# One SBUF tile shared from layer 0 to the tokens, whitening's sums taken in layer 0's last batch, 28 output stores, and keys written in order

## The chip, the cores and the metric

The kernel runs on one core of a Trainium2 chip. A core has TensorE (PE), VectorE (DVE), ScalarE (ACT), GpSimd (POOL) and SyncE (SP), each with its own instruction stream, and 16 DMA engines that the streams feed through queues; nearly all transfers here are issued by SP. The metric is the time of one execution on the device in microseconds. The kernel before takes 7492.99 us, the median of 3 runs between 7485.9 and 7499.06 us.

## The reference, cut to what matters

The input is 8 images of 56x56 pixels with 128 channels, all float32, and four layers follow one another:

```python
# layer 0: deformable convolution and an MLP, both with residuals
xp = x @ w_in + b_in
h = gelu(batch_norm(depthwise3x3(x)))
offset = h @ w_off + b_off ; mask = softmax(h @ w_msk + b_msk)
x = x + gamma1 * layer_norm(dcn(xp, offset, mask) @ w_out + b_out)
x = x + gamma2 * layer_norm(gelu(x @ w_fc1) @ w_fc2)
# layer 1: whitening. The flat activations become 64 rows; every 9th column is a sample
x1 = transpose(x).reshape(64, -1) ; x1_s = x1[:, ::9]
cov = x1_s @ x1_s.T / n_cols + 0.01 * eye(64)
y = isqrt_newton_schulz(cov, 5) @ (x1 - mean(x1_s))
# layer 2: attention (8 heads of 16, keys = queries = values) and 64 experts
t = t + attn(layer_norm(t)) ; t = t + experts(layer_norm(t))
# layer 3: linear attention and 64 experts
```

In layer 1 the reference names the array's axes N, C, H, W although they hold 8, 56, 56 and 128. So "rows of a block" are image rows: the 64 rows of `x1` gather image rows of all eight images, and nothing of the covariance is known before all of layer 0 has its result.

## The kernel before, in words

**Layer 0, first stage** (`conv_layer`, L127). Its instructions stand in the order they are written in (`manual_schedule`). For each image it loads the pixels (`xs`), transposes them, projects them (`pj`), filters them, and stores the projected strips to DRAM; one image later it computes the offsets and masks `om` from `hT` and stores them (L337); one image after that `ranged` (L341) runs ReLU over the offsets twice, once for each sign, into the scratch tile `over`, and gathers whether any offset is beyond 1 (`far`). After eight images one flag `near` is read, and an `If` takes the sampler for near offsets.

**Layer 0, second stage** (`sample_near`, L413). The loop over `g` has `LEN = PH + 5 = 12` ticks for each image. The MLP of the current image goes through a pipeline of six steps, one strip row `r` (of seven) a tick: `project` in tick r, ..., `combine` in tick r + 5. Beside it the next image's samples are made. In the last batch there is no next image. After the last strip of an image `by_patch(..., store=True)` writes the image to `z` in DRAM in 8 stores (L757). `z` is kept as [row, image, column, channel]. The big buffers of this stage (`wide`, `wT`, `hat`, `even`, `smp`) are tiles of their own.

**Layer 1** (`whiten_layer`, L1019). 14 loads bring all of `z` into `x` [128, 25088]: partition p < 64 holds the first half of row p of `x1`, partition 64 + p the second half. PE transposes samples (`p_smp`, L1063), DVE copies them, PE multiplies them into `cov` (L1073), and DVE sums the samples for the mean (`tot`, L1051). Then come `a` (L1094), its norm, five Newton-Schulz steps of 64x64 matmuls with copies on DVE (L1119 to L1129), and the subtraction of the mean from `x` in seven pieces of 3584 columns (L1140). For each piece PE multiplies by `both`, a block diagonal of two copies of the result (L1146), DVE and ACT copy the products to `o`, and 16 stores write it to `y` (L1157), each with 8 partitions that lie 8 apart, because neighbouring rows of a block go to different images.

**Token constants** (`token_layers`, L2663): weights are loaded and transposed, and `key_bound` (L2616) bounds the scores of layer 3.

**Keys** (`attention_keys`, L1191). The order here is the scheduler's. Zeros are written to the two DRAM arrays `sel_d` in 8 stores on ACT's queue (L1205). For each image the tokens `t` are loaded (L1166), normalised (`bn_stats` L1223, `rsqrt`, `normalize` L111), transposed to `xT` (L120), multiplied into the keys `kT` (two stores, L1250) and the values `va` (two stores, L1266); GpSimd squares the values, and DVE finds the largest norm, `tops`. From this `low` and the flag `small` follow, and the attention (`attend`, L1424) starts after the flag is read by all engines.

The change replaces these lines in the stage order:

```python
        # whiten_layer, before
        for c in range(0, WHALF, WC):
            for h in range(2):
                nc.sync.dma_start(
                    x[h * WB : (h + 1) * WB, c : c + WC],
                    zf[:, h * WHALF + c : h * WHALF + c + WC],
                )
        # attention_keys, before
        for sel in sels:
            rows = sel.rearrange("(r s) o -> r (s o)", s=S)
            for a in range(0, n_b * E, 128):
                nc.scalar.dma_start(rows[a : a + 128], zero)
```

Of the kernel before, what the change touches and what calls it, by code (L numbers as in the profile page):

```python
# [126 lines left out]
def conv_layer(tc, k, x, w, z):  # L127
# [3 lines left out]
    with ExitStack() as ctx:  # L131
# [7 lines left out]
        q.om = dp.tile([n_batch, T, NT, 3 * GP], F32, name="om_d")  # L139

# [36 lines left out]
        far = cp.tile([T, 2 * n_batch], F32, name="far")  # L177
        near = cp.tile([1, 1], I32, name="near")
        with ExitStack() as pre:
# [57 lines left out]
            xss, accs = {}, {}  # L237

            def load(n):
                xss[n] = hp.tile([T, NT, C], F32, name="xs")  # L240
                nc.sync.dma_start(
                    xss[n],
                    x[n].rearrange("h w c -> (h w) c").rearrange("(t p) c -> p t c", p=T),
                )
# [65 lines left out]
            def activated(n):  # L310
                hT = hp.tile([C, PH, PX, T // NX, NX], F32, name="hT")
                a4 = accs.pop(n).rearrange("p (a r) (b s) -> p r a b s", r=PH, s=PX)
                for r in range(PH):
                    nc.scalar.activation(
                        hT[:, r].rearrange("p s a b -> p a b s"),
                        a4[:, r],
                        AF.Gelu,
                        bias=bn_t,
                        scale=bn_s,
                    )  # L320
                return hT
# [18 lines left out]
            def ranged(n, om):  # L340
                for i, sign in enumerate((1.0, -1.0)):  # L341
                    over = ip.tile([T, NT, 2 * GP], F32, name="over")
                    nc.scalar.activation(
                        over,
                        om[:, :, : 2 * GP],
                        AF.Relu,
                        bias=minus1,
                        scale=sign,
                        accum_out=far[:, 2 * n + i : 2 * n + i + 1],
                    )  # L350

            with tc.manual_schedule(engines=None):
                load(0)
                oms = {}
                for n in range(n_batch + 2):
                    if n + 1 < n_batch:
                        load(n + 1)
                    if n < n_batch:
                        pj = hp.tile([IH, IW, C], F32, name="pj")
# [8 lines left out]
                    if n > 1:  # L368
                        ranged(n - 2, oms.pop(n - 2))
                    if 0 < n <= n_batch:  # L370
# [13 lines left out]
        with both.Else():  # L384
            with tc.For_i(0, n_batch) as n:
                sample_any(tc, k, q, x, n)

# [25 lines left out]
def sample_near(tc, k, q, n_batch):  # L413
# [4 lines left out]
    with ExitStack() as ctx:  # L418
# [11 lines left out]
        wide = bp.tile([T, NT * WS], F32, name="wide")  # L430
# [4 lines left out]
        wT = bp.tile([KP, T, GRP, NT], F32, name="wT")  # L435
# [11 lines left out]
        even = wp.tile([C, C], F32, name="even")  # L447
# [11 lines left out]
        def weights(n):  # L459
# [6 lines left out]
            for r0 in range(0, PH, 2):  # L466
# [4 lines left out]
                hat = rp.tile([T, 2, NP, 2 * PX, 3, GRP], F32, name="hat")  # L471
                hat = hat[:, :, :, :n_t]
# [203 lines left out]
        blocks = (1, 1, 1, 2, 2)  # L676
        for g in range(LEN * n_batch):
            n, tick = divmod(g, LEN)
            more = n + 1 < n_batch
            if more and tick == 2:  # L680
# [19 lines left out]
            if five:  # L700
                fn, r = five
                combine(xts[fn][:, r], p5, rs5, xts[fn][:, r])
                if r == PH - 1:
# [26 lines left out]
            if left > 1:  # L730
                sample(n + 1, m + 16)

# [76 lines left out]
def sample_any(tc, k, q, x, n):  # L809

    nc = tc.nc
    with ExitStack() as ctx:
# [12 lines left out]
        xt = bp.tile([T, PH, GT, C], F32, name="xt")  # L825
        by_patch(nc, q.x[n], xt)
        zt = bp.tile([T, PH, GT, C], F32, name="zt")
# [191 lines left out]
def whiten_layer(tc, k, z, y):  # L1019

    nc = tc.nc
    n_half = -(-WCOLS // WSTEP) // 2
    first = (0, -WHALF % WSTEP)
    n_tr = -(-n_half // 128)
    WC = 7 * 512
    zf = z.rearrange("h n w c -> (h n w c)").rearrange("(r s) -> r s", r=WB)
    with ExitStack() as ctx:
# [4 lines left out]
        ps1 = ctx.enter_context(tc.tile_pool(name="l1p1", bufs=1, space=PSUM))  # L1032
        ps2 = ctx.enter_context(tc.tile_pool(name="l1p2", bufs=2, space=PSUM))


        x = bp.tile([2 * WB, WHALF], F32, name="x")
        for c in range(0, WHALF, WC):
            for h in range(2):
                nc.sync.dma_start(
                    x[h * WB : (h + 1) * WB, c : c + WC],  # L1040
                    zf[:, h * WHALF + c : h * WHALF + c + WC],
                )


        smp = bp.tile([128, 2 * n_tr * WB], F32, name="smp")
        cov = ps1.tile([WB, WB], F32, name="cov")
        tot = bp.tile([2 * WB, 1], F32, name="tot")
        n_mm = 0
        for h in range(2):
            rows = slice(h * WB, (h + 1) * WB)  # L1050
            nc.vector.tensor_reduce(  # L1051
                tot[rows],
                x[rows, first[h] : first[h] + WSTEP * (n_half - 1) + 1 : WSTEP],
                AX.X,
                ALU.add,
            )
            for i0 in range(0, n_tr, 8):
                p = ps.tile([128, 8, WB], F32, tag="m", name="p_smp")
                m = min(8, n_tr - i0)
                for i in range(i0, i0 + m):  # L1060
                    n = min(128, n_half - i * 128)
                    a = first[h] + i * 128 * WSTEP
                    nc.tensor.transpose(  # L1063
                        p[:n, i - i0, :],
                        x[rows, a : a + WSTEP * (n - 1) + 1 : WSTEP],
                        k.ident[rows, rows],
                    )
                for i in range(i0, i0 + m):
                    n = min(128, n_half - i * 128)
                    at = (h * n_tr + i) * WB  # L1070
                    s = smp[:n, at : at + WB]
                    nc.vector.tensor_copy(s, p[:n, i - i0, :])
                    nc.tensor.matmul(  # L1073
                        cov, s, s, start=(n_mm == 0), stop=(n_mm == 2 * n_tr - 1)
                    )
                    n_mm += 1

        n_smp = float(2 * n_half)
        fold = bp.tile([2 * WB, 2, WB], F32, name="fold")
        for h in range(2):  # L1080
            nc.vector.tensor_tensor(
                fold[:, h], k.ident[:, :WB], k.ident[:, WB:], ALU.add
            )
        p = ps.tile([2 * WB, 1], F32, tag="m", name="p_mean")
        nc.tensor.matmul(
            p, fold.rearrange("p a b -> p (a b)"), tot, start=True, stop=True
        )
        mean = bp.tile([2 * WB, 1], F32, name="mean")
        nc.vector.tensor_scalar(mean, p, 1.0 / n_smp, None, ALU.mult)

        a = bp.tile([WB, WB], F32, name="a")
        ieps = bp.tile([WB, WB], F32, name="ieps")
        nc.vector.tensor_scalar(ieps, k.ident[:WB, :WB], WEPS, None, ALU.mult)
        nc.vector.scalar_tensor_tensor(a, cov, 1.0 / n_smp, ieps, ALU.mult, ALU.add)  # L1094


# [4 lines left out]
        ones = bp.tile([WB, WB], F32, name="ones")  # L1101
        nc.vector.memset(ones, 1.0)
        p = ps.tile([WB, 1], F32, tag="m", name="p_norm")
        nc.tensor.matmul(p, ones, ssum, start=True, stop=True)
        norm = bp.tile([WB, 1], F32, name="norm")
        nc.scalar.activation(norm, p, AF.Sqrt)
        inv = bp.tile([WB, 1], F32, name="inv")
        nc.vector.reciprocal(inv, norm)
        rinv = bp.tile([WB, 1], F32, name="rinv")
        nc.scalar.activation(rinv, norm, AF.Sqrt)  # L1110
        nc.vector.reciprocal(rinv, rinv)
        i15 = bp.tile([WB, WB], F32, name="i15")
        nc.vector.tensor_scalar(i15, k.ident[:WB, :WB], 1.5, None, ALU.mult)
        ym = sp.tile([WB, WB], F32, tag="ym", name="ym")
        nc.vector.tensor_scalar(ym, a, inv, None, ALU.mult)
        zm = k.ident[:WB, :WB]
        for _ in range(WITER):
# [4 lines left out]
            p = ps2.tile([WB, WB], F32, tag="ns", name="p_y")  # L1122
            nc.tensor.matmul(p, ym, tm, start=True, stop=True)
            ym = sp.tile([WB, WB], F32, tag="ym", name="ym")
            nc.vector.tensor_copy(ym, p)
# [4 lines left out]
        dm = bp.tile([WB, WB], F32, name="dm")  # L1130
        nc.vector.tensor_scalar(dm, zm, rinv, None, ALU.mult)
        both = bp.tile([2 * WB, 2 * WB], F32, name="both")
        nc.vector.memset(both, 0.0)
        nc.vector.tensor_copy(both[:WB, :WB], dm)
        p = ps2.tile([2 * WB, WB], F32, tag="ns", name="p_low")
        nc.tensor.matmul(p[WB:], k.ident[:WB, :WB], dm, start=True, stop=True)
        nc.vector.tensor_copy(both[WB:, WB:], p[WB:])

        for c in range(0, WHALF, WC):
# [13 lines left out]
            for h in range(2):  # L1153
                k_, off = divmod(h * WHALF + c, IW * C)
                for b in range(NB):
                    row, n = divmod(7 * b + k_, NB)
                    nc.sync.dma_start(  # L1157
                        y[n]
                        .rearrange("(a r) w c -> r a (w c)", r=7)[row][:, off : off + WC],
                        o[h * WB + b : (h + 1) * WB : NB],  # L1160
                    )
# [29 lines left out]
def attention_keys(tc, k, w, yv, kT_out, va_out, low, bias, small, sels):  # L1191


# [3 lines left out]
    n_b = yv.shape[0]  # L1197
    with ExitStack() as ctx:
        cp = ctx.enter_context(tc.tile_pool(name="akc", bufs=1))
        zero = cp.tile([128, S], F32, name="edge")  # L1200
        nc.gpsimd.memset(zero, 0.0)
        for sel in sels:
            rows = sel.rearrange("(r s) o -> r (s o)", s=S)
            for a in range(0, n_b * E, 128):
# [1678 lines left out]
```

## Time and profile before

| What | us | Where it is read |
|---|---|---|
| median of 3 runs (lowest, highest) | 7492.99 (7485.9, 7499.06) | times |
| the profiled execution: its own time, its span | 7509.97, 7508.2 | times, page |
| layer 0, first stage | 0 to 395 | timeline |
| flag, weights and `om` of image 0 | 395 to 460 | timeline |
| layer 0, second stage | 460 to 1460 | timeline |
| last image to `z`, `z` to `x`, covariance | 1460 to 1545 | timeline |
| Newton-Schulz and subtraction | 1545 to 1567 | timeline |
| products and 112 stores | 1567 to 1684 | timeline |
| constants, first tokens, statistics | 1684 to 1740 | timeline |
| keys and values of 8 images | 1740 to 2052 | timeline |
| attention and all that follows | 2052 to 7508 | timeline |

The chain of work that ended last runs mostly through the attention: 54% of the span is PE, and the three costliest lines of the chain (L1527, L1587, L1603) are the attention's. The stages that the change touches lie before 2052 us, and each ends before the next begins: the covariance needs the last image, the stores need the matrix, the tokens need the last store, and the attention needs the flag from the last keys. In the views below "start, us" is the begin and length of an instruction or a group of equal ones; "x112" counts them; SPq and ACTq are the instructions with which SP and ACT issue transfers, so their time is the time of issuing, which is long when the queue is full.

### The profile page before, as it was taken

The page shows a single profiled execution, that of the slowest core. Times are in us where ns is not written, and L with a number is a line of the kernel's source. Part 1 is how long each engine was busy: PE and PEld are TensorE (multiplying, and loading weights), DVE is VectorE, ACT ScalarE, POOL GpSimd, SP SyncE. Part 2 cuts the span into 40 slices and gives each one's busy share as a digit, 9 for nine tenths or more (in the row PEclk, how much of TensorE's full clock was granted, in tenths as well). Part 3 has the DMA queues.
Part 4 walks back from the last instruction along what each step waited for, and adds up shares of the span by engine and source line. Part 5 has one row for each costly group of instructions (what it writes and reads, how often), then busy time and mean ns, then how long its engine had stood idle before and what let it go on. Part 6 is the DMA issues. An engine that isn't in the chain of part 4 may idle for free.

```text
span 7508.2 us, 162711 instructions
## 1 busy us (share of the span) xinstructions
PE 6513.2 (87%) x63686; PEld 3041.6 (41%) x63686; DVE 4668.4 (62%) x8268; ACT 4337.6 (58%) x5268; POOL 3898.1 (52%) x3925
## 2 busy tenths in 40 slices
PE   7938888745699999998999998999998999689668
PEld 5626556423433333332333333333333333267326
DVE  5757775126756677676777676776675777446542
ACT  4525455302277777776777776777776776424320
POOL 0003233202267677667666767767766767335650
PEclk8858888866799999999999999999998999789775
DMA  5533435346467677766777766767765767752227
GB/s 134 140 68 72 87 73 95 65 107 233 189 158 187 164 164 190 168 165 153 175 165 177 178 162 142 191 160 177 179 162 135 190 161 181 206 175 89 78 87 223
DMA packets 721075, 1126.49 MB, mean 150 GB/s; under 512 B 106225, under 2 KB 472514, under 8 KB 711362
## 3 DMA queue, kind: packets, MB, share of 16 engines
q1 hardware_dynamic: 676946, 1073.74, 58.5%
q10 hardware_dynamic: 39248, 37.88, 1.5%
q8 instruction: 513, 8.40, 0.5%
q0 software_dynamic: 4096, 4.24, 0.2%
q14 instruction: 272, 2.23, 0.1%
HBM read 292.59 MB, written 193.65 MB: 65 GB/s over the span
## 4 chain that ended last, share of the span: by engine, by line
PE 54%; POOL 7%; DMA 4%; DVE 3%; issue 2%; SPq 1%; ACT 1%; ACTq 0%; POOLq 0%; DVEq 0%
PE p_s L1527 20%; PE av L1587 15%; PE p_t L1603 11%; POOL t_all L1578 3%; POOL t_all L1573 2%; PE p_s L2340 1%; DVE t_all L1562 1%; DMA room<-in_L_ffn_weight_dram 1%; PE p_qk L2409 1%; PE p_o L1665 1%; DMA sel_d<-vals,row 1%; SPq L1575 1%; PE p_g L1714 1%; DMA t_all<-t_all 1%; POOL xn L2545 1%
## 5 line engine op out<-in xcount | busy, mean ns | idle before, releaser
L1538 ACT ACTIVATE room<-p_s,bias 128x1024 f32<-128x1024 f32 (+2 forms) x3008 | 3142.1, 1102 | 1153.3 <-PE p_s L1527 1149.7
L1562 DVE STREAM_TRANSPOSE t_all<-room 128x1024 f32<-128x1024 f32 x1920 | 2246.7, 1217 | 751.1 <-ACT room L1538 293.1
L1578 POOL COPY t_all<-t_all 32x1024 f32<-32x1024 f32 x1920 | 1988.7, 1036 | 104.1
L1527 PE MATMUL p_s<-t_all 32*128 32x512 f32 x10752 | 1647.6, 642 | 14.6 <-DMA t_all<-kT_d 13.7
L1573 POOL COPY t_all<-t_all 32x1024 f32<-32x1024 f32 x960 | 995.7, 1037 | 1142.0 <-DVE t_all L1562 857.4
L1527 PEld LDWEIGHTS p_s<-t_all 32*128 32x128 f32 x10752 | 502.5, 183 | 1147.3 <-issue 512.4
L1587 PE MATMUL av<-room,vas 128*32 128x512 f32 (+1 forms) x7616 | 820.0, 518 | 5.1 <-issue 3.3
L1587 PE MATMUL av<-room 128*32 128x512 f32 (+1 forms) x6208 | 663.1, 516 | 1.9 <-issue 1.2
L1603 PE MATMUL p_t<-t_all,vas 128*32 128x256 f32 x8064 | 546.8, 389 | 47.4 <-POOL t_all L1578 45.1
L1603 PE MATMUL p_t<-t_all,room 128*32 128x256 f32 x7296 | 492.3, 387 | 39.4 <-POOL t_all L1578 29.7
L1603 PEld LDWEIGHTS p_t<-t_all,vas 128*32 128x32 f32 x8064 | 215.0, 110 | 503.9 <-issue 249.4
L1603 PEld LDWEIGHTS p_t<-t_all,room 128*32 128x32 f32 x7296 | 194.3, 109 | 455.3 <-issue 235.8
L1587 PEld LDWEIGHTS av<-room,vas 128*32 128x32 f32 x7616 | 204.6, 111 | 216.2 <-issue 112.6
L512 PE MATMUL p_w<-ident,wide 112*88 112x112 f32 x896 | 152.3, 316 | 132.4 <-DVE wide L502 84.3
L581 POOL TENSOR_TENSOR rsy<-rsy,mhalf 112x4 f32<-112x4 f32 x56 | 58.0, 1035 | 386.2 <-DVE rsy L580 386.2
L1587 PEld LDWEIGHTS av<-room 128*32 128x32 f32 x6208 | 160.0, 110 | 187.1 <-issue 105.4
L1622 DVE TENSOR_TENSOR acc<-acc,p_t 128x256 f32<-128x256 f32 x320 | 132.4, 414 | 134.0 <-PE p_t L1603 131.7
L431 POOL MEMSET wide<- 112x10416 f32 x1 | 8.8, 8777 | 394.4 <-DMA om_d<-om 394.4
L512 PEld LDWEIGHTS p_w<-ident,wide 112*88 112x88 f32 x896 | 124.8, 172 | 201.5 <-issue 131.5
L618 PE MATMUL p_f<-x1T,w 128*128 128x448 f32 x448 | 189.2, 565 | 16.9 <-ACT sqm L565 13.7
L514 ACT COPY wT<-p_w 88x448 f32<-88x448 f32 x152 | 137.2, 924 | 114.1 <-PE p_w L512 114.1
L306 DVE SCALAR_TENSOR_TENSOR acc<-xp,dw,acc 128x3136 f32<-128x3136 f32 x56 | 195.2, 3485 | 2.0
(369 smaller groups left out, 8585.2 us busy)
## 6 DMA issues: line engine op xcount, KB each, us to landing
t_all<-t_all SPq DMA_DIRECT2D x4800, 128.0 KB
px<-strips SPq DMA_DIRECT2D x64, 616.0 KB
room<-in_L_ffn_weight_dram SPq DMA_DIRECT2D x30, 1024.0 KB
room<-in_L_ffn_weight_dram SPq DMA_DIRECT2D x120, 256.0 KB
va_d<-va SPq DMA_DIRECT2D x16, 1600.0 KB
kT_d<-kT SPq DMA_DIRECT2D x16, 1568.0 KB
t_all<-kT_d SPq DMA_DIRECT2D x96, 256.0 KB
vas<-va_d SPq DMA_DIRECT2D x52, 256.0 KB
```

The lines of the kernel that those rows point to most:

```text
L306: nc.vector.scalar_tensor_tensor(acc, view(j), dw[:, j : j + 1], acc, ALU.mult, ALU.add)
L512: nc.tensor.transpose(p[:, g], around[:, :, g], k.ident[:T, :T])
L514: copy(wT[:, :, :, t].rearrange("k a g -> k g a"), p)
L618: nc.tensor.matmul(p, q.w1[:, f * 128 : (f + 1) * 128], x1T, start=True, stop=True)
L1527: nc.tensor.matmul(ss[j // 2][:m, j % 2, u * width : (u + 1) * width], key_tile(b.n, b.g, t, j), q[32 * j : 32 * j + 32], start=True, stop ...
L1538: nc.scalar.activation(e[:m, :, cols], s[:m, :, cols], AF.Exp, bias=bias[:m])
L1562: nc.vector.transpose(x[:, :, a, 2 * h : 2 * h + 2].rearrange("p q h b f -> p (h b) q f"), e.rearrange("p h (b q f) -> p (h b) q f", b=4, ...
L1573: nc.gpsimd.tensor_copy(dst, src)
L1578: nc.gpsimd.tensor_copy(into[r, u], x[r, u])
L1587: nc.tensor.matmul(av[32 * j : 32 * j + 32, :width], value_tile(b.n, b.g, t, j), es[j // 2][:m, j % 2, u * width : (u + 1) * width], start ...
L1603: nc.tensor.matmul(p[32 * j : 32 * j + 32, : QB // 2], value_tile(b.n, b.g, 4 * b.j + c, j), yt[:, :, :, j, c].rearrange("p q a f -> p a q ...
L1622: nc.vector.tensor_tensor(to, to, p, ALU.add)
```

## The change: what it does

- One tile `arena` [128, 25088] lives from layer 0 to the end. It holds `pj`, `xs` and one `hT` in the first stage, `wide`, `wT`, `hat` and `even` in the second, whitening's `x`, the buffers of keys and values, and then the tokens `t_all`. `ranged` works in place on the offsets: Abs, then ReLU with the bias of -1.
- The zeros for `sel_d` are written in the first stage, one store with each of the images 1 to 8, on SP's queue, from a tile of 448 columns read seven times.
- A class `WhitenSums` replaces the first half of whitening. In ticks 0 to 3 of the last batch SP issues the loads of images 0 to 6 from `z` into `arena` (56 loads of 8 rows, of 28672 or 14336 bytes a row). Image 7 is not stored; `take` moves its strip rows from `xt` to `arena` from SBUF to SBUF after each `combine` (8 transfers, 16 for r = 3). In ticks 6 to 11 `more` transposes the samples of one column group at the start of the tick and multiplies those of the group before into `cov`, which has a 65th column of ones so that it holds the sums too. The last group and the copy to `sums` follow the loop.
- `whiten_layer` is called after the token constants. It subtracts the mean as before, drops the last `p_y`, copies `ym` on ACT, and permutes the output rows with `order`, so that one store covers m images: 28 stores, four for each piece, of 8m neighbouring partitions to (m, 8) places in DRAM, m between 1 and 7.
- `attention_keys` stands in written order. The statistics of image n + 1 are taken among the groups of image n, the normalisation is split between DVE and ACT, four `kT` buffers take turns, the values are made in groups of four tiles with the squares on ACT, and the tokens of image n + 2 are loaded at the end of image n, after its two key stores.

```diff
 def ranged(n, om):
-    for i, sign in enumerate((1.0, -1.0)):
-        over = ip.tile([T, NT, 2 * GP], F32, name="over")
-        nc.scalar.activation(
-            over,
-            om[:, :, : 2 * GP],
-            AF.Relu,
-            bias=minus1,
-            scale=sign,
-            accum_out=far[:, 2 * n + i : 2 * n + i + 1],
-        )
+    part = om[:, :, : 2 * GP]
+    nc.scalar.activation(part, part, AF.Abs)
+    nc.scalar.activation(
+        part, part, AF.Relu, bias=minus1, accum_out=far[:, n : n + 1]
+    )
...
                     if n > 1:
                         ranged(n - 2, oms.pop(n - 2))
+                    if 0 < n and edges:
+                        rows = edges.pop().rearrange("r (a b) -> r a b", b=QC)
+                        nc.sync.dma_start(
+                            rows, empty.unsqueeze(1).to_broadcast([128, S // QC, QC])
+                        )
...
+        sums = WhitenSums(tc, k, q)
         for g in range(LEN * n_batch):
             n, tick = divmod(g, LEN)
             more = n + 1 < n_batch
+            if not more:
+                for i in range(2 * tick, min(2 * tick + 2, n_batch - 1)):
+                    sums.fetch(i)
+                if tick == 5:
+                    sums.begin(pst, "t", xp, "px")
+                if tick > 5:
+                    sums.more(ps, "m", tick - 6)
...
-                if r == PH - 1:
+                if fn == n_batch - 1:
+                    sums.take(fn, r, xts[fn][:, r])
+                elif r == PH - 1:
                     by_patch(nc, q.z[fn], xts.pop(fn), store=True)
...
+        sums.more(ps, "m", PH - 1)
+        sums.end()
+class WhitenSums:
+    def place(self, r, n):
+        return r + (r + n) // PH, (r + n) % PH
+    def fetch(self, n):
+        for r in range(PH):
+            for rows, at, a, m in self.parts(n, r):
+                self.nc.sync.dma_start(
+                    self.x[rows, at : at + m], self.q.zr[r, n][:, a : a + m]
+                )
...
+    def more(self, ps, tag, col):
+        for group in self.pieces((col + 1) * IW * C):
+            p = ps.tile([128, 7, WB], F32, tag=tag, name="p_smp")
+            for i, (h, a, last, n) in enumerate(group):
+                rows = slice(h * WB, (h + 1) * WB)
+                nc.tensor.transpose(
+                    p[:n, i], self.x[rows, a:last:WSTEP], self.k.ident[rows, rows]
+                )
+            nc.vector.tensor_copy(s[:n, :m, :WB], p[:n, :m])
+            self.add()
+            self.waiting.append((s, group))
...
 # whiten_layer
             for h in range(2):
-                k_, off = divmod(h * WHALF + c, IW * C)
-                for b in range(NB):
-                    row, n = divmod(7 * b + k_, NB)
-                    nc.sync.dma_start(
-                        y[n]
-                        .rearrange("(a r) w c -> r a (w c)", r=7)[row][:, off : off + WC],
-                        o[h * WB + b : (h + 1) * WB : NB],
-                    )
+                col, off = divmod(h * WHALF + c, IW * C)
+                cut = h * WB + 8 * (7 - col)
+                for lo, hi, n, at, j in (
+                    (cut, (h + 1) * WB, 0, col, 0),
+                    (h * WB, cut, col + 1, 55 * (col + 1) + col + 2, 5),
+                ):
+                    m = (hi - lo) // 8
+                    if m:
+                        dst = yu[at : at + 55 * m].rearrange("(n j) e -> n j e", j=55)
+                        nc.sync.dma_start(
+                            dst[:, j : j + 50 : 7, off : off + WC], o[lo:hi]
+                        )
...
 # attention_keys, under manual_schedule
+        load(0)
+        load(1)
+        for g in range(NG):
+            sums(0, g)
+        roots(0)
+        xn = norm(0, 0)
+        for n in range(n_b):
+            for g in range(NG):
+                turn(xn, xT, g)
+                if g:
+                    keys(n, xT, g - 1)
+                if g + 1 < NG:
+                    xn = norm(n, g + 1)
+                sums(n + 1, g)
+                if g > 1:
+                    values(n, xT, 4 * (g - 2), square)
+            roots(n + 1)
+            keys(n, xT, NG - 1)
+            values(n, xT, 4 * (NG - 2), square)
+            if n + 1 < n_b:
+                xn = norm(n + 1, 0)
+            values(n, xT, 4 * (NG - 1), square)
+            load(n + 2)
+            for g in range(2):
+                nc.sync.dma_start(va_out[n, g], vas[n % 2][:, g].rearrange("p t j d -> p (t j d)"))
```

## The prediction

> **What bounds the kernel now.** I read four views. The page first: its chain of waits and costliest groups belong to the attention (L1527, L1587), whose instructions the change leaves as they are. From the first read of `small` on, all five engines have the same sequence in both programs, so what is won or lost falls before 2052 us and stays. Then the timeline of the same 2052 us, for the anchors; then the windows, for what each stage is full of; then the groups of single lines. Timeline (start, length, instruction):
>
> ```profile
> 394.82 0.34 SPq L337 DMA_DIRECT2D om_d<-om  x1
> 1371.21 97.77 SPq L757 DMA_DIRECT2D z<-xt  x13
> 1472.51 29.26 SPq L1039 DMA_DIRECT2D x<-z  x14
> 1576.33 104.44 SPq L1157 DMA_DIRECT2D y<-o  x112
> 1688.76 7.58 SPq L1166 DMA_DIRECT2D t<-y  x2
> ```
>
> Each of these releases the next stage. The windows (length, busy time of PE, PEld, DVE, ACT, POOL with counts, clock, DMA share, GB/s):
>
> ```profile
> 1424.00:1460.00 36.00, 32.10 (x147) 19.68 (x145) 8.53 (x34) 16.74 (x29) 10.98 (x10) 0.99 0.01 2
> 1460.00:1536.00 76.00, 10.72 (x72) 8.62 (x72) 9.84 (x39) 0.00 (x0) 0.00 (x0) 0.50 0.91 191
> 1567.00:1685.00 118.00, 53.56 (x100) 22.12 (x100) 15.17 (x26) 15.99 (x28) 0.00 (x0) 0.73 0.45 112
> 1685.00:1740.00 55.00, 3.65 (x10) 1.63 (x10) 17.73 (x127) 0.00 (x0) 19.51 (x9) 0.50 0.84 296
> 1800.00:2045.00 245.00, 171.22 (x703) 114.85 (x701) 189.66 (x602) 69.40 (x166) 61.61 (x12) 0.78 0.56 207
> ```
>
> The reader is to see four things. The last MLP ticks are PE's (32 of 36 us) while DMA is idle. Bringing `z` to `x` is DMA's (0.91). The stage of the 112 stores is limited by transfers of 112 GB/s, although the engines' share is only 0.45. In the keys DVE is the fullest (190 of 245 us).
>
> **The change part by part.** Anchors are of the profiled execution (its own time 7509.97 us; span 7508.2). It lies 17 us above the median of the runs; I add the sum to that median.
>
> *First stage.* The eight zero stores have 0.3 to 1 us of issue each on SP and 1.6 MB; in the page's first two slices DMA is half idle (5 and 5 tenths), a load is issued one image ahead of use, and on ACT's queue each took 4.97 us. Cost 0; without that cover 8 x 5 = 40 us. `ranged` for image 7 used to run beside the store of `om`, which lands at 401.3. In place it must wait for it: 401.3 + Abs 1.97 + ReLU 1.97 + 0.2 + 1.0 for the flag = 406.5, against 400.0, with the `If` released at 401.3 before: **+5 to +6.5 us**, I take 6.5.
>
> *Fetch.* SP issues it after image 6's last store (1378.5 + 6.5 = 1385). It is 11.24 MB, 8 partitions a transfer, 8 apart. The nearest row is `y<-o`: same partitions, same row length, 12.8 MB in 107 us (1576 to 1684) = 121 GB/s at 8 packets in flight. So 93 us, to 1478. Bounds: 213 GB/s, as `x<-z` with 64 partitions, gives 53 us; 107 GB/s gives 105. Queued behind it on SP is `take` of strip 0, 2 us, and its landing. PE meets `more(0)` at the head of tick 6, 1417.2 + 6.5 = 1424; its transposes wait for that landing, and behind them on PE stand all matmuls of ticks 6 to 11, and ACT, DVE and POOL behind those. PE goes on at about 1484 (bounds 1444, 1496): 60 us of wait in a stage where it was busy.
>
> *Rest of the batch.* From tick 6 to the last `combine` is 42.2 us in the trace (1417.2 to 1459.5). I add 3 for the clock, which rows after a pause show at 0.50 for 4 to 10 us; 9 for 44 transposes (0.17 to 0.25 each) and their passes (0.11 to 0.31 each) now on PE's path; 7.5 for waits on `take` (about 2 us landing at some of the six ticks, twice at the 16 transfers of r = 3); 12.5 for the last `take`, `more` and the copy. Sums ready at 1484 + 42 + 3 + 9 + 7.5 + 12.5, rounded 1560. Before, `cov` was ready at 1543.8. The removed 8 stores (9.5 us), 14 loads (59 us) and `tot` (two of 5.1 us) are thus more than eaten up by the wait: **+16**.
>
> *Constants.* They ran in the shadow of the last stores and of the tokens' loads (1680.9 to 1693.8); now, on DVE, `kb_top` and `bound` stand ahead of `a` in the queue, and the loads only start after the `If`. Same chain: 12.9 us, plus 15 small DVE copies of 0.15 to 0.2 = 16. `a` at 1577 (before 1545.5). Newton and the seven subtractions (2.07 us each, now interleaved alike) 22 us; last `p_y` gone, 1 us: first product at 1599, first store at 1608 (before 1576.3): **+32 in all so far**.
>
> *Stores.* The same 12.85 MB in 896 rows of 14336 B. No row shows a transfer to (m, 8) places. Lower bound: 16 packets in flight at the 420 GB/s of `kT` would be 31 us, then PE's 47 us for 49 products (53.6 busy) decides. Nearest row: `y<-o` itself, 107. Upper: packets in flight followed the outer count in every row that I can see (8 for `y<-o`, 14 for `z<-xt`, 16 for 64 partitions). The outer count here is m, from 1 to 7, so if it holds a store keeps m streams of 8 rows: 24 stores x 8 + 4 x 1 = 196 rows one after another on the first stream, at 535 ns (fastest packet) 105 us, at 914 (mean) 179. I take 125: fewer streams meet than in `y<-o`, so packets run at some 640 ns, nearer the fast end. Landed at 1608 + 125 + 2 = 1735, before 1684.
>
> The Trainium skill ("DMA: Bandwidth & Descriptors", section "Why a DMA increments its semaphore by 16 and not by 1") says that a queue spreads a transfer over the largest k up to 16 that divides the slowest non-1 dimension of both sides, on the lowest-numbered engines. The trace's 8, 14 and 16 agree. By it the first engine would carry 196 rows and the stage takes 105 us or more; the row of `y<-o` alone would give 107, and thus some 18 us less in the total than my sum.
>
> *First tokens.* Before: 1684 to 1740 for constants, two loads and edges that shared the queue (`sel_d` 33 us, the first statistics at 1707, the first transpose at 1740.2). Now only the load (8.5), 28 x 0.26 = 7.3 of statistics, 5.3 for the root on POOL, 0.7: first transpose at 1735 + 22 = 1757, before 1740.2. So 34 of the lost us come back here: **+17**.
>
> *Keys.* Before 311 us from the first transpose to `low`, 38 an image. New, image by image: from the last key (E) the two key stores take 7.8 us on the DMA engines, the tokens of image n + 2 lie behind them (7.2 + 2), so they land at E + 17. DVE runs in order: it has some 7 us of work, then meets their `bn_stats`, and `norm` and the keys of the next group stand behind those. Then six groups at 3.2 us (DVE: 4 x 0.26, 2 x 0.31, 0.68, half a copy and the gaps), then `ms` waits 6.3 us for the root on POOL (4.80) with the last key copy behind it: 17 + 19 + 6.3 = 43 an image (bounds 39 and 47). The first image needs no late load, 27.5; the last 34.5. 27.5 + 6 x 43 = 286, + 34.5 = 320, against 311: **+9**. What is saved, GpSimd's squares and seven small value copies, lies beside DVE and is worth nothing while this wait stands; without it an image takes 32 us.
>
> Sum: 6.5 + 9.5 (sums at 1560) + 16 (constants) + 18 (stores) + 1 (landing) - 34 + 9 = +26; 7493 + 27 = **7520 us**.
>
> **Rivals.** *A, the stores run wide.* All 16 streams, PE decides: 47 instead of 125, -78: 7442. For it: 8m neighbouring partitions, as the loads with 64 have 16 in flight. Against: the destination's outer count. *B, the load is not late, on the other side.* The mechanism is only the keys' DVE wait: it goes if the tokens land by E + 7, that is if the loads of 7.2 us overlap the key stores rather than follow; 32 an image, -66: 7454. It decides alone once an image is under 39 us (-24 or more). For it: the DMA share in the keys is 0.56, and two images are held. Against: one queue, where the trace's `t<-y` issued after stores took them in order. *C, fetch at the rate of `x<-z`:* -40, 7480. *D, packets meet:* 179 for the stores, or 47 an image: +54 or +24, 7545 to 7574. *E, nothing gained or lost:* stores as before (107) and an image at 42: -24, 7496, within what a measurement can tell.
>
> **How the numbers follow.** Forecast as summed (7508 to 7550): 0.43. A 0.12, B 0.14, C 0.08, D 0.15, E 0.08. A measurement of this kernel can tell some 0.2%, 15 us, from no change (the runs before spread by 13). Faster: A, B and half of C, 0.30. Same: E, and the other half of C, 0.12. Slower: 0.58. Range: A's 7442 and two small gains together at the low end, D at the high: 7430 to 7590; the likeliest case's own is 7505 to 7560.
>
> **What would show it.** In the profile after: a PE gap of about 60 us at the head of tick 6, with the transposes of `p_smp` behind a DMA (right), or none over 20 (C); `a` some 30 us later; 28 stores over 105 to 160 us with few packets in flight, or under 60 (A); DVE waiting for `t<-y` some 10 us in each image, with images 43 us apart, or 32 (B). I would be wrong most easily in the stores' rate and in the keys, where two waits in order on DVE are worked out and not seen.

## The result, and the profile after

The changed kernel takes 7540.41 us (median of 5 runs, 7533.65 to 7554.67) against 7496.19 for the kernel before in 5 runs (7485.9 to 7503.89): slower by 44 us, a ratio of 1.0063 with a 95% interval from 1.0048 to 1.0077. The forecast was 7520, 24 above that median. The profiled execution has a span of 7537.9 us.

The timeline of SP, whose transfers release the stages (start, length, instruction):

```profile
380.83 0.34 SPq L360 DMA_DIRECT2D om_d<-om  x1
393.03 3.39 SPq L911 DMA_DIRECT2D xt<-in_x_dram  x8
1369.99 82.71 SPq L808 DMA_DIRECT2D arena<-z  x54
1453.35 106.21 SPq L817 DMA_DIRECT2D arena<-xt  x64
1612.01 93.33 SPq L1276 DMA_DIRECT2D y<-o  x28
1731.95 4.37 SPq L1283 DMA_DIRECT2D t<-y  x2
```

The reader is to see that SP issues the loads of images 0 to 6 until 1452.7 and only then the 64 strip transfers of image 7 (`arena<-xt`, until 1559.6), where PE was to finish layer 0 beside them. The strips fill 106 us although one takes 0.70 to 0.89 us to issue: between the rows SP waits for the next `combine`. The timeline of PE shows at each column group what the head of the tick waited for (in brackets: idle before, and what ended it):

```profile
1466.67 0.92 PE L870 MATMUL p_smp<-ident,arena 64*128 64x64 f32 x6 [57.94 <-DMA arena<-xt]
1480.96 0.87 PE L870 MATMUL p_smp<-ident,arena 64*128 64x64 f32 x6 [0.60 <-DMA arena<-xt]
1495.01 0.92 PE L870 MATMUL p_smp<-ident,arena 64*128 64x64 f32 x6 [3.39 <-DMA arena<-xt]
1514.52 0.57 PE L870 MATMUL p_smp<-ident,arena 64*128 64x64 f32 x3 [5.84 <-DMA arena<-xt]
1531.70 0.92 PE L870 MATMUL p_smp<-ident,arena 64*128 64x64 f32 x6 [2.56 <-DMA arena<-xt]
1546.49 0.92 PE L870 MATMUL p_smp<-ident,arena 64*128 64x64 f32 x6 [6.12 <-DMA arena<-xt]
1561.99 0.92 PE L870 MATMUL p_smp<-ident,arena 64*128 64x64 f32 x6 [10.55 <-DMA arena<-xt]
```

One wait of 57.9 us, and then one in every tick, because the strip that the tick needs was made by the tick before. SP's timeline between 1486 and 1494 us shows what that takes for one strip:

```profile
1486.14 6.50 SPq L817 DMA_DIRECT2D arena<-xt  x8
```

The eight transfers are issued from 1486.1 to 1492.6, and PE goes on at 1495.0, 8.9 us after the first; for the 16 transfers of r = 3 it is 12.9 us (1501.6 to 1514.5). The windows (columns as before: length, busy time of PE, PEld, DVE, ACT, POOL, clock, DMA share, GB/s) show both, then the stores and the keys:

```profile
1412.00:1467.00 55.00, 0.33 (x3) 0.36 (x4) 0.00 (x0) 0.00 (x0) 0.00 (x0) 0.50 0.43 109
1467.00:1566.00 99.00, 69.94 (x313) 47.85 (x312) 14.82 (x50) 18.30 (x31) 13.14 (x12) 0.71 0.06 15
1612.00:1732.00 120.00, 44.14 (x83) 18.19 (x81) 12.45 (x18) 13.66 (x24) 11.76 (x6) 0.69 0.29 107
1790.00:2055.00 265.00, 152.32 (x632) 93.69 (x632) 145.97 (x507) 107.62 (x226) 28.77 (x6) 0.77 0.52 183
```

In the first row PE, DVE, ACT and POOL stand still. In the second PE's clock is 0.71, where the same ticks before had 0.99. The stores move 107 GB/s, with less DMA share than before. In the keys DVE is no longer full (146 of 265 us, before 190 of 245), and yet the stage takes longer. The view of waits between 1780 and 2090 us (waiter, what it waited for, total us, times, longest) says why:

```profile
DVE st L1351 <- DMA t<-y: 64.6, 6, 10.9
DVE ms L1360 <- POOL rs L1472: 34.9, 7, 5.0
```

By anchors, forecast against measured, in us:

| Step | forecast | profile after |
|---|---|---|
| first transposes of layer 0, against 37.39 before | no change | 29.16 |
| last `om` store to weights of the second stage (before 6.65) | 13.2 | 12.2 |
| PE's wait at tick 6 | 60 | 57.9 |
| from its end to the sums | 74 | 99.6 |
| sums to `a` | 16 | 14.3 |
| `a` to the first store | 31 | 31.4 |
| first store to the tokens' load | 127 | 119.9 |
| from there to the first transpose of the keys | 22 | 25.8 |
| first transpose to `low` and `small` (before 311.6) | 320 | 333.6 |

`small` is set at 2091.3, before at 2051.8: 39.5 later. Counted from the last `om` store (380.83, before 394.82) it is 53.5 later. The rest, the same instructions, took 9.8 less in this execution. Such differences are scatter: in profiles of kernels with an equal first stage the last `om` store is issued between 380.3 and 400.6. So steps are compared here by the distance of two anchors, and kernels by the ratios of their runs.

### The profile page after: what moved, and what is told of

Same layout as the page of the kernel before. It is cut to its first block, busy times and chain, and to the rows that moved or that the text cites. A ratio compares the mean times of both kernels' runs of the same rounds, so it can differ in the third digit from the quotient of the medians.

```text
span 7537.9 us, 162656 instructions
## 1 busy us (share of the span) xinstructions
PE 6507.4 (86%) x63686; PEld 3026.0 (40%) x63686; DVE 4601.4 (61%) x8052; ACT 4396.2 (58%) x5368; POOL 3863.1 (51%) x3918
## 5 line engine op out<-in xcount | busy, mean ns | idle before, releaser
L1739 DVE STREAM_TRANSPOSE arena<-room 128x1024 f32<-128x1024 f32 x1920 | 2246.7, 1217 | 744.0 <-ACT room L1715 351.5
L1755 POOL COPY arena<-arena 32x1024 f32<-32x1024 f32 x1920 | 1993.7, 1038 | 104.3
L1704 PE MATMUL p_s<-arena 32*128 32x512 f32 x10752 | 1649.8, 643 | 17.1 <-DMA room<-va_d 16.2
L1750 POOL COPY arena<-arena 32x1024 f32<-32x1024 f32 x960 | 997.8, 1039 | 1126.8 <-DVE arena L1739 869.0
L1704 PEld LDWEIGHTS p_s<-arena 32*128 32x128 f32 x10752 | 502.9, 184 | 1152.6 <-issue 520.0
L1780 PE MATMUL p_t<-arena,vas 128*32 128x256 f32 x8064 | 546.9, 389 | 44.6 <-POOL arena L1755 41.3
L1780 PE MATMUL p_t<-arena,room 128*32 128x256 f32 x7296 | 492.7, 387 | 37.6 <-POOL arena L1755 23.6
L1780 PEld LDWEIGHTS p_t<-arena,vas 128*32 128x32 f32 x8064 | 215.0, 109 | 500.5 <-issue 247.0
L1780 PEld LDWEIGHTS p_t<-arena,room 128*32 128x32 f32 x7296 | 194.6, 109 | 456.2 <-issue 243.7
L552 PE MATMUL p_w<-ident,arena 112*88 112x112 f32 x896 | 151.6, 315 | 132.9 <-DVE arena L542 81.5
L554 ACT COPY arena<-p_w 88x448 f32<-88x448 f32 x152 | 137.1, 923 | 111.2 <-PE p_w L552 111.2
## 6 DMA issues: line engine op xcount, KB each, us to landing
arena<-arena SPq DMA_DIRECT2D x4800, 128.0 KB
```

The lines of the kernel that those rows point to most:

```text
L552: nc.tensor.transpose(p[:, g], around[:, :, g], k.ident[:T, :T])
L554: copy(wT[:, :, :, t].rearrange("k a g -> k g a"), p)
L1704: nc.tensor.matmul(ss[j // 2][:m, j % 2, u * width : (u + 1) * width], key_tile(b.n, b.g, t, j), q[32 * j : 32 * j + 32], start=True, stop ...
L1739: nc.vector.transpose(x[:, :, a, 2 * h : 2 * h + 2].rearrange("p q h b f -> p (h b) q f"), e.rearrange("p h (b q f) -> p (h b) q f", b=4, ...
L1750: nc.gpsimd.tensor_copy(dst, src)
L1755: nc.gpsimd.tensor_copy(into[r, u], x[r, u])
```

## The experiments

The theory is the forecast's own: PE's wait for the loads, strips that land too late, DVE's wait for late tokens and the constants on the path cost more than the change saves, and the stores gain nothing. The rivals are that transfers set the end wherever PE's instructions stand, that behind each wait another stands, and that the stores' shape is at fault. All ratios are to the kernel before on the same chip; the changed kernel's is 1.0063. A gain over the changed kernel, given in us, is the difference of two such ratios, and with their intervals it is sure to some 16 us either way.

### All transposes behind the loop

```diff
-                if tick > 5:
-                    sums.more(ps, "m", tick - 6)
...
-        sums.more(ps, "m", PH - 1)
+        for i in range(PH):
+            sums.more(ps, "m", i)
```

> The transposes and covariance passes of all seven column groups stand behind the loop instead of at the head of ticks 6 to 11. If PE's wait for the loads (57.9 us at tick 6) and the seven waits for strips that come only after the tick before (some 33 us of the 99.6 from there to the sums) are the cost, the MLP ends near 1451 as before, the 64 strip transfers follow the loads on SP at 0.77 us each, 1453 to 1502, and the sums are ready near 1512 instead of 1566: 50 us faster than the changed kernel, 7490. Rival: the transfers set the end whatever PE does; then the sums stay within 10 us of 1566 and the time at 7535.

Ratio 0.9995 (0.9979 to 1.001), 51 us below the changed kernel, and the sums at 1521.9. SP's timeline:

```profile
1371.15 84.55 SPq L807 DMA_DIRECT2D arena<-z  x56
1456.82 58.22 SPq L816 DMA_DIRECT2D arena<-xt  x64
```

The loads take as long as before. The strips now go out back to back, 58 us instead of 106, since their contents are ready. The order of PE's queue was worth 51 us. The sums were expected at 1512: the strips took 58 us where 49 were put. SP's 64 strips now stand last before the sums, which the run with image 7 by way of DRAM puts to the test.

### One tick later

```diff
-                if tick > 5:
-                    sums.more(ps, "m", tick - 6)
+                if tick > 6:
+                    sums.more(ps, "m", tick - 7)
...
-        sums.more(ps, "m", PH - 1)
+        for i in range(PH - 2, PH):
+            sums.more(ps, "m", i)
```

> The transposes of column group c stand at the head of tick c + 7 instead of c + 6, the last two groups behind the loop; the transfers are as in the changed kernel. This tells the one long wait (57.9 us) from the seven landings. PE still meets the loads, one tick on, and waits some 48 us there, but each strip then has a whole tick to land. If the landings that come right after the tick's own combine are the larger part, the sums are ready near 1525, as in the run with all groups behind the loop (1521.9), ratio 1.000. Rival: the long wait is what is lost, and hardly less of it here; then the sums stay near 1555, ratio 1.005.

Ratio 1.0011 (0.9997 to 1.0025): 39 of the 51 us come back although the long wait stays. PE's timeline:

```profile
1473.85 0.92 PE L871 MATMUL p_smp<-ident,arena 64*128 64x64 f32 x6 [52.80 <-DMA arena<-xt]
1486.21 0.90 PE L871 MATMUL p_smp<-ident,arena 64*128 64x64 f32 x6
1495.64 0.90 PE L871 MATMUL p_smp<-ident,arena 64*128 64x64 f32 x6
1512.78 0.87 PE L871 MATMUL p_smp<-ident,arena 64*128 64x64 f32 x6 [0.80 <-DMA arena<-xt]
1520.02 0.92 PE L871 MATMUL p_smp<-ident,arena 64*128 64x64 f32 x6 [4.51 <-DMA arena<-xt]
1526.66 0.92 PE L871 MATMUL p_smp<-ident,arena 64*128 64x64 f32 x6 [4.23 <-DMA arena<-xt]
```

52.8 us of waiting still stand at the head, but the next ticks have no wait before them; two waits of 4.5 and 4.2 us are left, ahead of the last two groups. From the end of the long wait to the sums it is 57 us (1473.9 to 1531.1) instead of 99.6, and the clock over it is 0.83 instead of 0.71. So the strips' issue and landing within a tick are the larger part of what could be had by moving `more` alone; the long wait's time is mostly not to be had that way, because without it the sums come only some 10 us earlier: loads and strips on SP then set the end.

### Image 7 by way of DRAM

```diff
-                if fn == n_batch - 1:
-                    sums.take(fn, r, xts[fn][:, r])
-                elif r == PH - 1:
+                if r == PH - 1:
                     by_patch(nc, q.z[fn], xts.pop(fn), store=True)
...
+        sums.fetch(n_batch - 1)
+        for i in range(PH):
+            sums.more(ps, "m", i)
```

> As the run with the late transposes, and image 7 goes to DRAM and back like the other seven (8 stores, 8 loads) in place of the 64 transfers from SBUF to SBUF. In that run SP issued those 64 from 1456.8 to 1514.3, 0.77 us each and back to back behind the loads, and the sums followed at 1521.9. If that issuing is what set its end, then here the image is stored by 1464, loaded by about 1480, and the sums are ready near 1493: some 28 us below that run, 0.9955 to 0.997 of the kernel before. Rival: the landing of any small transfer, not the number issued, sets the end: within 8 us of that run, 0.9985 to 1.000.

Ratio 0.9973 (0.9958 to 0.9989), 0.0022 below the run with all transposes behind the loop, and the sums at 1495.2, two us from the expectation. The ratio lies just above the expected band, whose edge is inside its interval, but that interval and the other run's overlap. The traces part the two: from the first load of SP to the sums it is 150.8 us there (1371.15 to 1521.9) and 128.0 here (1367.16 to 1495.2), 23 us less. SP issues the 8 stores and 8 loads between 1454.5 and 1472.8, 18 us in place of 58. The way through DRAM that the change had saved is shorter than 64 small transfers. That SP's time to issue them was the cost fits both runs; as number, size and kind of the transfers changed together, the number alone is not shown.

### Tokens loaded early

```diff
                     xn = norm(n, g + 1)
+                if g + 1 == NG - 1:
+                    load(n + 2)
                 sums(n + 1, g)
...
-            load(n + 2)
```

> The tokens of image n + 2 are loaded after the last normalisation of image n, ahead of its key and value stores on the queue. If the late load is the cost, DVE's six waits of 10.8 us (64.6 in all) go, an image takes some 34 us instead of 44.4, and the time is 60 us below the changed kernel, 7480. Rival: another wait stands right behind (the root on GpSimd 5 us, keys on PE, the stores of keys and values holding their buffers); then an image stays over 40 us and the gain is under 25, 7515 or more.

Ratio 0.9981 (0.9963 to 0.9998), 62 us below the changed kernel, as expected; the keys take 271.8 us (1763.5 to 2035.3) instead of 333.6. SP's timeline, two images:

```profile
1818.73 0.34 SPq L1283 DMA_DIRECT2D t<-y  x1
1828.63 0.33 SPq L1402 DMA_DIRECT2D kT_d<-arena  x1
1829.02 0.42 SPq L1402 DMA_DIRECT2D kT_d<-kT  x1
1829.62 2.08 SPq L1450 DMA_DIRECT2D va_d<-arena  x2
1852.95 0.34 SPq L1283 DMA_DIRECT2D t<-y  x1
1862.86 0.82 SPq L1402 DMA_DIRECT2D kT_d<-arena  x2
```

The load goes out 10 us ahead of the key stores, not behind them, and images are 34.2 us apart (1828.63 to 1862.86), against 44.4. DVE's wait for `t<-y` is gone from the view of waits. One line's place is worth more than the whole loss.

### The root's multiplication later

The early load, and the `ms` of `roots` in a function of its own:

```diff
+        def shifts(n):
...
+            ms = bp.tile([T, NT], F32, name="ms")
+            nc.vector.scalar_tensor_tensor(ms, mv[:, :, 0], -1.0, rs, ALU.mult, ALU.mult)
...
             values(n, xT, 4 * (NG - 2), square)
+            shifts(n + 1)
             if n + 1 < n_b:
```

> The early load of tokens, and DVE's multiplication that waits for the root on GpSimd (4.98 us, seven times) stands behind the last keys and values of the image instead of ahead of them. If the wait is on the path, an image goes from 34 to some 30 us: 28 us below the run with the early load alone, 0.9945. Rival: the first normalisation of the next image needs the root anyhow and only the keys move: less than 10 us, 0.997.

Ratio 0.9978 (0.996 to 0.9996), the keys 272.8 us: no gain, and the rival is right. The waits with the early load alone, and then with this:

```profile
DVE ms L1360 <- POOL rs L1473: 34.9, 7, 5.0
PE p_tr L120 <- DVE xn L111: 60.0, 14, 4.7
```

```profile
DVE ms L1366 <- POOL rs L1481: 30.8, 7, 4.4
PE p_tr L120 <- DVE xn L111: 55.7, 14, 4.1
```

The wait hardly shrinks, and PE waits for the next image's `xn` behind it in both. The first normalisation needs the root; what stands ahead of it in DVE's queue is not what binds.

### Stores: 112 of 8 neighbours, and the 112 of the kernel before

The first writes each store image by image; the second goes back to partitions 8 apart, and `ident` for `order`.

```diff
-                        nc.sync.dma_start(
-                            dst[:, j : j + 50 : 7, off : off + WC], o[lo:hi]
-                        )
+                        for i in range(m):
+                            nc.sync.dma_start(
+                                dst[i, j : j + 50 : 7, off : off + WC],
+                                o[lo + 8 * i : lo + 8 * i + 8],
+                            )
```

> 112 output stores again, each of 8 partitions that are neighbours, where before they lay 8 apart and the changed kernel's 28 stores take 8m neighbours. If a transfer uses as many streams as its outer count (8 here, m = 1 to 7 in the 28) and neighbours do not slow one another down, packets run at 535 ns in 8 streams: 896 / 8 x 0.535 = 60 us, then issuing 112 stores at about 0.6 us = 67 us decides, instead of 120: some 50 us below the changed kernel, 7490. Rival: 8 streams meet as in the kernel before at 914 ns, whatever the partitions: 107 us, gain 13, 7527.

```diff
-                p[h * WB : (h + 1) * WB], zm, order, start=True, stop=True
+                p[h * WB : (h + 1) * WB], zm, ident, start=True, stop=True
...
+                for b in range(NB):
+                    row, n = divmod(7 * b + k_, NB)
+                    nc.sync.dma_start(
+                        y[n]
+                        .rearrange("(a r) w c -> r a (w c)", r=7)[row][:, off : off + WC],
+                        o[h * WB + b : (h + 1) * WB : NB],
+                    )
```

> The 112 output stores of the kernel before (8 partitions, 8 apart) in the changed kernel, without the permutation. In 112 stores of 8 neighbours the packets ran at 977 ns with 8 in flight, 123 us, no better than the 120 of the 28. If any set of 8 is held to some 120 GB/s, this takes 107 as in the kernel before and the change of the stores as such costs 13 us: 7538 on the first chip, a ratio of 1.0045. Rival: what the 28 stores cost is in the rest of the stage, and it stays at 118 or more: 1.006.

With neighbours the ratio is 1.0057 (1.004 to 1.0073), no gain; with the old stores 1.0053 (1.0037 to 1.0069), 8 us, which the intervals do not part from nothing. SP's timeline tells more, neighbours first:

```profile
1632.77 119.67 SPq L1277 DMA_DIRECT2D y<-o  x112
```

```profile
1623.44 105.95 SPq L1270 DMA_DIRECT2D y<-o  x112
1732.82 4.24 SPq L1279 DMA_DIRECT2D t<-y  x2
```

From the first store to the tokens' load: 119.9 us with 28 stores, 123.0 with 112 neighbours (1632.8 to 1755.7), 109.4 with the old ones. Worked out from the records of the packets: the 28 stores had 2 to 7 packets in flight for most of the stage (4.7 on average) at 627 ns on average (median 535), the 112 neighbours up to 8 (7.2) at 980, the old stores in the kernel before up to 8 (7.7) at 914. The product moves little: all three are between 105 and 121 GB/s. With neighbours both the expectation (60 to 67 us) and its rival (107) missed. The bound of 60 us for 8 streams at 535 ns falls: packets were slower where more ran beside them. Neighbours do not help; they took 14 us more than partitions 8 apart. With the old stores the stage is near the expected 107, and the ratio lies between the expectation and its rival. Why 12.85 MB to these places are held to that rate stays open.

### Constants beside Newton's steps

```diff
+            whiten_layer(tc, k, arena, st, y)
             wkT = transposed(nc, k, cp, rp, ps, a["L2_attn_W_k"], "wkT")
...
-        whiten_layer(tc, k, arena, st, y)
         attention_keys(
```

> Whitening's instructions are placed ahead of the transposes and bounds of the token constants, whose loads stay where they are. If the constants on the path cost what the trace shows (14.1 us from the sums to a), a follows the sums within 2 us and the constants run beside Newton's steps: 12 us below the changed kernel, 7528. Rival: they only move to another place on the path (DVE between Newton's steps, or ahead of the first tokens): less than 4 us.

Ratio 1.005 (1.0035 to 1.0064), 10 us below, not clear of the intervals. `a` follows the sums after 8.2 us instead of 14.3 (expected: within 2), but from `a` to the first product it is 24.5 instead of 22.7: 4 us on the path by the trace. Part of the constants moved to between Newton's steps, as the rival has it.

### The zero stores back in the keys

```diff
-                    if 0 < n and edges:
-                        rows = edges.pop().rearrange("r (a b) -> r a b", b=QC)
...
+        zero = cp.tile([128, S], F32, name="edge")
+        nc.gpsimd.memset(zero, 0.0)
+        for sel in sels:
+            rows = sel.rearrange("(r s) o -> r (s o)", s=S)
+            for a in range(0, n_b * E, 128):
+                nc.scalar.dma_start(rows[a : a + 128], zero)
```

> The eight zero stores back on ACT's queue at the start of the keys, out of the first stage. If they cost nothing in the first stage, om of image 0 is back within 3 us of the changed kernel's time (428.4), and the first tokens and the first image's stores share the engines with 12.5 MB: K0 10 to 30 us later, ratio 1.008 to 1.010. Rival: in the first stage they hold SP's queue ahead of loads and stores; then that stage ends 5 to 15 us earlier and the total is as the changed kernel's, 1.005 to 1.007.

Ratio 1.0076 (1.0052 to 1.0101). `om` of image 0 is back at 428.6 against 428.4: in the first stage these stores cost nothing that could be seen, though one execution of each, with the scatter above, would not show a few us. In the keys they do not delay the first transpose (25.0 us after the tokens' load is issued, against 25.8), but the first image's key stores (45.8 us after it, against 31.0), and the stage takes 348 instead of 334. The place was expected wrongly, the sum about right.

### What pays, together

Image 7 by DRAM with the transposes behind the loop, the early load, the 112 old stores, and the constants beside Newton's steps.

> Image 7 by DRAM with the transposes behind the loop (0.9973 of the kernel before, 0.0090 below the changed kernel's 1.0063), the early load (0.9981, 0.0082 below), the 112 stores of the kernel before (1.0053, 0.0010 below) and the constants beside Newton's steps (1.0050, 0.0013 below). The four lie one after another, so they add: 1.0063 - 0.0195 = 0.987, some 98 us under the kernel before, with the sums near 1495, the stores 107 to 110 and images of 34 us. Rival: what one gains another takes (the early load or the stores meeting the constants' loads): 0.990 or more.

7400.81 us (median), a ratio of 0.9852 (0.9829 to 0.9875): faster than both kernels, by 1.5% than the one before. SP's timeline, and the window of its keys:

```profile
1373.45 83.53 SPq L806 DMA_DIRECT2D arena<-z  x56
1458.62 11.97 SPq L907 DMA_DIRECT2D z<-xt  x8
1474.75 5.22 SPq L806 DMA_DIRECT2D arena<-z  x8
1545.23 105.69 SPq L1268 DMA_DIRECT2D y<-o  x112
```

```profile
1700.00:1960.00 260.00, 174.77 (x785) 108.57 (x783) 172.30 (x570) 132.81 (x280) 34.15 (x11) 0.84 0.62 234
```

The sums are ready at 1503.4 (1543.8 before; some 8 us later than expected), the first transpose of the keys is at 1681.3 (1740.2), and `small` at 1953.9, 98 us ahead of the kernel before. The parts add up: 0.987 was expected, inside the interval.

## Why the prediction was right

The direction, the places and most of the sizes held; the loss was 44 us where 24 to 27 were forecast (the forecast's terms make 26, and 27 were added). That the total came this near is in part luck. From the last `om` store to `small` the change cost 53.5 us in the profiled executions, twice the forecast's sum; against it stood a first stage that ended 14 us earlier, 8 of them at its start and the rest perhaps scatter, and that the forecast did not have. With the measured sizes of the table in place of the forecast's own (+25.6 for the rest of the batch, +13.6 for the keys, +3.8 for the first tokens, -7.1 for the stores, -8.2 for the first transposes, -4.4 for the others) the sum comes to some 7543 us, and 7540 was measured.

- *Fetch and PE's wait.* Right: 57.9 us of wait for 60. By the records of the packets the 11.24 MB moved from 1369.4 to 1463.0, at 120 GB/s, for the 121 taken from the old stores. The rival C, the fetch at 213 GB/s, is refuted. What the forecast did not say is that taking this wait away alone gains little, because SP's strips end the stage next.
- *Rest of the batch.* This term was mis-sized: 99.6 us for 74. The forecast gave 7.5 for waits on strips and 3 for the clock. PE's waits on strips after the first are 29.1 us, 10.55 of them in what the forecast counted as the last `take`, `more` and copy, so 18.5 stand against the 7.5. The forecast counted a landing of about 2 us; SP's issue of 8 transfers, 6.5 us in each tick, and of 16, 11.9, it left out. The clock stood at 0.71 over the stretch, and PE was busy 69.9 us where, by estimate, the 38.9 that it was busy in the same ticks before and the forecast's 9 for the samples make 48: 22 for the 3. Moving the samples by one tick brought 39 us back, the waits and the clock together: that shows the strips that a tick waits for as the cause.
- *Constants.* Right: 14.3 for 16. That this can all be had back by another order is not shown; 4 us were.
- *Stores.* Right in total: 119.9 for 127, with packets at 627 ns for the 640 forecast. The reason, few streams that each run near the fastest packet, agrees with the median of 535 ns, but is not shown by a run. The Trainium skill's rule on the engines of a transfer ("DMA: Bandwidth & Descriptors", section "Why a DMA increments its semaphore by 16 and not by 1") agrees with what is seen: mostly 2 to 7 packets in flight for outer counts of 1 to 7, and up to 8 for a count of 8; the records do not name the engines. But what the first experiment on the stores took from it, that more streams would be faster, did not follow: 8 neighbours took 123 us. Rival A, at 47 us, is refuted.
- *First tokens.* 25.8 for 22. A tile's statistics came every 0.40 us, not every 0.26: in the written order each `bn_aggr` stands right behind the `bn_stats` whose result it takes, where the scheduler's order had another `bn_stats` between them. That this order is the cause is read from the two timelines and was not tested.
- *Keys.* The mechanism is as forecast: six waits of 10.8 us for tokens behind the key stores, an image 44.4 us for 43 (with the first image 31.0 for 27.5, hence 333.6 for 320), and the early load brings it to 34.2 (forecast without the wait: 32). Rival B described what the early load made. The second part of the argument, that `ms` holds up the last keys and costs 6.3 an image, did not hold as put: moving it gained nothing, since the next image's normalisation waits for the same root.
- *First stage.* The flag came 5.6 us later against its store (forecast 6.5), and no cost of the zero stores could be seen, as said. Missed was a gain of 8 us: the first load of pixels is issued at 19.06 instead of 28.06. Before, SP waited 8.6 us there for the stores from `edge`, a tile of the set-up; that the old `xs` shared its memory is read from the order of the pools and was not tested.

## What to carry to other kernels

Work put into an idle engine's gap must be placed in its queue where its data are ready, not where the gap begins: at the head of a tick it held up everything behind it. A load for the batch after next belongs ahead of this batch's stores on the same queue, once its buffer is free; here that one line was worth 62 us. Few large transfers need not be faster than many: here 28 stores took 120 us, and the 112 of the kernel before, put in their place, 109. Many small ones keep the issuing engine busy: count what it needs, 0.77 us each here, wherever something waits for the last of them.

## What was not expected of the hardware

Stores of 14336 bytes a packet to rows of `y` ran at 108 GB/s with 4.7 packets in flight at 627 ns on average, at 106 with up to 8 at 980 from partitions side by side, and at 121 with up to 8 at 914 from partitions 8 apart. And 64 transfers within SBUF of 28 KB or less each took SP 0.70 to 0.89 us to issue, so that with a trip of the whole image through DRAM, 8 stores and 8 loads, the sums came 23 us earlier, counted from the first load.
